# A decoder layer on one core: tile-wise waits, GpSimd diagonals and an earlier load where the opening meets the main loop

## The chip, the core and the metric

The kernel runs on one core of a Trainium2 chip. The metric is the device time of one launch in microseconds (us). The engines are TensorE (PE, with its weight loads, PEld), VectorE (DVE), ScalarE (ACT), GpSimd (POOL) and SyncE (SP), which here issues every DMA.

## What is computed

The input x has the shape 4 x 2048 x 512 (float32). The reference adds three branches to it, one after another, each on a layer norm of what came before:

```python
x = x + ssm(layernorm(x))      # y = 2 Re(z), z' = V (A z + Vinv dt x), scanned over the first axis (4 steps)
x = x + xattn(layernorm(x), ctx)   # 16 heads of 32, 77 context rows, softmax, Wq Wk Wv Wo
x = x + ffn(layernorm(x))      # W_exp (512 -> 2048), butterfly, exact gelu, butterfly, W_con (2048 -> 512)

def butterfly(y, weights, dim):          # 11 stages; stage s mixes i with i ^ 2**s
    for s in ...:
        a, b = the two halves of each pair
        y = stack(w00 * a + w01 * b, w10 * a + w11 * b)
```

The kernel folds W_exp and the first butterfly into one 512 x 2048 matrix, and the second butterfly and W_con into one of 2048 x 512. Both are then used in seven products instead of eight (Strassen's scheme in Winograd's form).

## The kernel before, in words

**Units.** The 2048 positions are cut into 16 units of 128, each with its 4 steps of the first axis, so a unit is a tile xt of 128 x 4 x 512. `front(u)` computes the first two branches and the last layer norm of a unit, as a generator of 50 steps; `feed_forward(u)` computes the third branch. In the main loop TensorE runs the products of `feed_forward(u)`, and after each of them `step()` (L649) may take a step of `front(u + 1)`: 50 steps over 102 of its 112 products.

**The up phase of a unit** has 8 pairs p of 7 products (L661, two matmuls each). TensorE's order for the first pairs is: pair 0's products 1, 6, 5 (`up_head`), then 2, 7 (`up_mid`); then for each further pair 1, 6, 5, the previous pair's 4, 3 (`up_tail`), and 2, 7. For unit 0 and p < 4 this order is fixed by hand. Product 1 of pair 0 needs only xnt; product 6 needs t2, which `combine` (L634 to L637) makes from xnt in the tile tb. Product 1 is copied out as p1 by ACT (L681), product 2 ends in a Gelu into a11 (L669, L693), product 7 in u3 and a22 (L696, L697). The weights of pair 0 are loaded in the opening (w_first, L840), those of the other pairs by L676 into one of three buffers in turn. At p = 1, x of unit u + 2 is loaded (L721). The down phase has 7 products of 8 parts each (L735).

**The opening** (L785 to L847) does three things at once: `_recurrence_taps` and `_keys_values` (small), `front(0)` (called `first`), and `_prepare` (called `prep`), which builds the two folded matrices. The order of TensorE, SyncE and GpSimd follows the program there, so the driver's `run(...)` calls and the loop at L829 set which step of `prep` goes beside which of `first`. In `_prepare`:

- `_low_products` (L186, GpSimd) and `diagonals` (L251, VectorE) make the operands of a butterfly's lower and upper stages: `bd` for the first (in the place of wo), `bdd` for the second, four of the 16 at a time between the products that need `bd`.
- L291, L303 and L315 are the TensorE stages for the first matrix. `evict` moves each bank from PSUM by VectorE (L245) or ACT (L247); six banks serve these stages in turn.
- Eight steps (L338 to L349) make the seven combinations of quarters: GpSimd L341, L342, VectorE L343, L344, and a store each (L345), with plain copies stored by L334.
- 16 steps with L355 (which reads `bdd`), then 16 with L365 and L375, make the second matrix in wdn. After every fourth of the latter, L384 to L387 combine into wup, and seven stores of 256 KB (L389) send the parts out as dn7: four sets, of which the last ends the opening. L378 loads a bias, and L391 adds it.

After `prep` x of unit 1 is loaded (L841 calls `load_x`, L418), and the biases ybias and db follow (L845, L846, added by L847 on GpSimd).

**Places.** The pool `prep` is closed at the end of the opening, and the pools of the main part (L848 to L852) take its room. In the built program, in bytes of a partition from the start of wup:

| prep | from | main part over it |
|---|---|---|
| wup, 32 KiB | 0 | x of unit 2 (xlast); a11, a12, a21 |
| wdn, 32 KiB | 32768 | a22, s1, u2d; weights 0 (pair 2); most of weights 1 (pair 3) |
| low_up, later low_dn, 15.9 KiB | 65568 | end of weights 1; tb, p1, u2, u3 |
| b1, b2, hp0 to hp3, hp_up, hp_dn | 81824 | weights 2 (pair 1), which also lie over the pool taps |

A pool opened in the place of another waits by default for all that the old pool held. Outside the opening and the fixed parts, a planner orders each engine's instructions: it goes by its own reckoning of when each will be ready, and by program order where several are. `keep_in_program_order` (keep) ties an instruction to its place among the others kept so on its engine.

Of the kernel before, what the change touches and what calls it, by code (L numbers as in the profile page):

```python
# [17 lines left out]
P = 128  # L18
# [5 lines left out]
NB = HID // P  # L24
# [142 lines left out]
def _low_products(nc, keep, low, transposed, shared):  # L167

    e, off = low[:, 0 : 2 * NB], 2 * NB
    for s in range(1, LOW):
        n = 2 ** s
        w = low[:, off : off + NB * 2 * n]
        off += NB * 2 * n
        parts = ((nc.gpsimd, slice(0, NB)),)
        if shared and s == LOW - 1:
            parts = (nc.vector, slice(0, NB // 2)), (nc.gpsimd, slice(NB // 2, NB))
        for engine, b in parts:
            v, old = (a.rearrange("p (b x) -> p b x", b=NB)[:, b] for a in (w, e))  # L180
            k = b.stop - b.start
            if transposed:
                v, old = v.rearrange("p b (x c) -> p b x c", c=2), old.unsqueeze(3).to_broadcast([P, k, n, 2])
            else:
                v, old = v.rearrange("p b (r x) -> p b r x", r=2), old.unsqueeze(2).to_broadcast([P, k, 2, n])
            keep(engine.tensor_tensor(v, v, old, ALU.mult))  # L186
        e = w
    return e.rearrange("p (b x) -> p b x", b=NB)
# [36 lines left out]
def _prepare(nc, keep, pool, room, late, banks, dram, ident, wexp_t, up_low, up_high, up_bias, dn_low, dn_high, wcon,  # L225
# [9 lines left out]
    highs, brw, spare = room  # L235
    brow = dram.tile([2, HID], F32, name="brow")
    t = wdn
# [8 lines left out]
        else:  # L246
            nc.scalar.copy(out, ps)  # L247

    def diagonals(hp, place, some=slice(0, NB)):
        for m in range(NB)[some]:  # L250
            keep(nc.vector.tensor_tensor(place[:, m, :].rearrange("p (b i) -> p b i", b=NB),  # L251
                                         hp[:, m, :].unsqueeze(2).to_broadcast([P, NB, sub]),
                                         mask.unsqueeze(1).to_broadcast([P, NB, sub]), ALU.mult))
        return [place[:, m, :] for m in range(NB)]
# [17 lines left out]
    hp = _regrouped(nc, keep, pool, hscr[0], _high_products(nc, pool, highs[:, 0], False), "hp_up")  # L272
    e = _low_products(nc, keep, low, False, True)
    hp_dn = _high_products(nc, pool, highs[:, 1], True)
    yield
    for g in range(4):
        ps = banks()
        for j in range(4):
            b = 4 * g + j
# [6 lines left out]
    for g in range(4):  # L286
        for c in range(NC):
            ps = banks()
            for j in range(4):
                b = 4 * g + j  # L290
# [5 lines left out]
    low = pool.tile([P, nlow], F32, tag="lowc", name="low_dn")  # L296
    keep(nc.sync.dma_start(out=low, in_=dn_low))
    hp_dn = _regrouped(nc, keep, pool, hscr[1], hp_dn, "hp_dn")
    bd = diagonals(hp, spare[:, 0 : NB * P].rearrange("p (m q) -> p m q", q=P))
    for m in range(NB):  # L300
        ps = banks()
        for c in range(NC):
# [2 lines left out]
        if m % 4 == 3:  # L305
            yield
    el = _low_products(nc, keep, low, True, False)
    pb = banks()
    place = late()
    for g in range(4):  # L310
        bdd = diagonals(hp_dn, place, slice(4 * g, 4 * g + 4))
        for c in range(NC):
            ps = banks()
            for j in range(4):
                nc.tensor.matmul(ps.rearrange("p (k m) -> p m k", m=4)[:, j], lhsT=t[:, 4 * g + j, c * P : (c + 1) * P],  # L315
                                 rhs=bd[4 * g + j], start=j == 0, stop=True, skip_group_check=True)
            evict(wup[:, c, :].rearrange("p (k m) -> p k m", m=NB)[:, :, 4 * g : 4 * g + 4], ps.rearrange("p (k m) -> p k m", m=4))
        for j in range(4):
            m = 4 * g + j
            nc.tensor.matmul(pb[:, m : m + 1], lhsT=bd[m], rhs=b2[:, m : m + 1], start=True, stop=True)  # L320
        nc.sync.dma_start(out=t[:, 4 * g : 4 * g + 4, :], in_=wcon.rearrange("(p m) d -> p m d", m=NB)[:, 4 * g : 4 * g + 4, :])
        yield
# [48 lines left out]
    for n, b in enumerate(order):  # L371
# [7 lines left out]
        if n % 4 == 3:  # L379
            f = slice(n // 4 * 2, n // 4 * 2 + 2)  # L380
# [15 lines left out]
def kernel(ctx: ExitStack, tc: tile.TileContext, x, ctx_t, ssm_vec, ssm_vt, ssm_vinv, wq_t, wk_t, wv_t,  # L396
                        wo_t, wexp_t, up_low, up_high, up_bias, dn_low, dn_high, wcon, b_con, down_bias, out):
    nc = tc.nc
# [17 lines left out]
    def load_x(u):  # L416
        xt = (xlast if u % 3 == 2 else xpool).tile([P, T, D], F32, tag=f"xt{u % 3}", name=f"xt{u}")
        tc.keep_in_program_order(nc.sync.dma_start(out=xt, in_=x[:, u * P : (u + 1) * P, :].rearrange("t p d -> p t d")))  # L418
        return xt

    def norm_stats(xt):

        st = small.tile([P, T, 6], F32, tag="st", name="st")
        mv = small.tile([P, T, 2], F32, tag="mv", name="mv")
        for t in (2, 3, 0, 1):
            nc.vector.bn_stats(st[:, t, :], xt[:, t, :])  # L426
            nc.vector.bn_aggr(mv[:, t, :], st[:, t, :])
        v = small.tile([P, T], F32, tag="v", name="v")
        vi = small.tile([P, T], I32, tag="vi", name="vi")
        y = small.tile([P, T], F32, tag="y", name="y")  # L430
        w = small.tile([P, T], F32, tag="w", name="w")
        nc.vector.tensor_scalar(v, mv[:, :, 1], LN_EPS, None, ALU.add)
        nc.vector.tensor_scalar(vi, v.bitcast(I32), 1, None, ALU.logical_shift_right)
        nc.vector.tensor_scalar(y.bitcast(I32), vi, -1.0, 1597463007.0, ALU.mult, ALU.add)
        nc.vector.tensor_scalar(v, v, -0.5, None, ALU.mult)
        for _ in range(3):
            nc.vector.tensor_tensor(w, y, v, ALU.mult)
            nc.vector.tensor_tensor(w, w, y, ALU.mult)
            nc.vector.scalar_tensor_tensor(y, w, 1.5, y, ALU.add, ALU.mult)
        return mv, y  # L440
# [21 lines left out]
            nc.scalar.copy(xnt[:, :, t, :], ps)  # L462
        res.append(xnt)

    def normed_pairs(xt, res):


        mv, y = norm_stats(xt)
        xpt = work.tile([P, T // 2, D // NS, P], F32, tag="xnt", bufs=2, name="xpt")
        half = D // 2  # L470
        yield
        rows = {}

        def row(n):
            i, h = divmod(n, 2)
            rows[n] = work.tile([P, NC, 2, NS], F32, tag="xn", name="xp")
            for k in range(2):
                t = 2 * i + k
                nc.vector.tensor_scalar(rows[n][:, :, k, :], xt[:, t, h * half : (h + 1) * half].rearrange("p (f n) -> p f n", n=NS),
                                        mv[:, t, 0:1], y[:, t : t + 1], ALU.subtract, ALU.mult)  # L480

        row(0)
        for n in range(T):
            i, h = divmod(n, 2)
            if n + 1 < T:
                row(n + 1)
            yield
            ps = psum.tile([P, NC, P], F32, tag="f", name="ps_t")
            for f in range(NC):
                nc.tensor.transpose(ps[:, f, :], rows[n][:, f, :, :].rearrange("p k n -> p (k n)"), ident)  # L490
            nc.scalar.copy(xpt[:, i, NC * h : NC * h + NC, :], ps)
        res.append(xpt)
# [17 lines left out]
    def front(u, xt, res, wq=None):  # L510


        got = []
        yield from normed_pairs(xt, got)
        xpt = got.pop()
        for c in range(NC):
            ps = psum.tile([P, T, P], F32, tag="f", name="ps_s")
# [122 lines left out]
    def feed_forward(u, xt, rhs, other):  # L640
# [4 lines left out]


        slot = [0]

        def step():  # L649
            slot[0] += 1  # L650
            for _ in range(slot[0] * 50 // 102 - (slot[0] - 1) * 50 // 102):
                next(other, None)

        def bank(tag):
# [71 lines left out]
        a, b, c, b7, a4 = (bank(g).rearrange("p (t d) -> p t d", t=2) for g in "abcba")  # L726
# [54 lines left out]
    xts = {}  # L781
# [3 lines left out]
    with ExitStack() as stack, tc.manual_schedule(engines={E.PE, E.SP, E.Pool}):  # L785
# [13 lines left out]
        def run(*gens):  # L799
            for g in gens:  # L800
                next(g, None)
# [6 lines left out]
        with tc.tile_pool(name="taps", bufs=1) as tp:  # L808
# [5 lines left out]
            first = front(0, xts.pop(0), ready, wq)  # L814
# [8 lines left out]
        run(prep, first, prep, first, prep, first, prep)  # L823
        nc.sync.dma_start(out=wq7, in_=wq)
        run(prep, prep, prep, prep)
        for _ in range(8):
            run(prep, first)
        run(first, first)
        for n, _ in enumerate(prep):  # L829
            if n not in (4, 8, 12, 22, 23, 24, 25, 26):  # L830
                next(first, None)
            if n == 3:
                quarter_loads(wo, wo_t, (0, 1, 2, 6))
                nc.gpsimd.tensor_tensor(wo[:, 4], wo[:, 6], wo[:, 0], ALU.subtract)
                nc.gpsimd.tensor_tensor(wo[:, 6], wo[:, 2], wo[:, 6], ALU.subtract)
                nc.gpsimd.tensor_tensor(wo[:, 5], wo[:, 2], wo[:, 4], ALU.subtract)
                nc.gpsimd.tensor_tensor(wo[:, 3], wo[:, 1], wo[:, 5], ALU.subtract)
            if n == 17:
                early.append(work.tile([P, 7, 2, P], F32, tag="pt", bufs=1, name="w_first"))
                nc.sync.dma_start(out=early[0], in_=up7[0])  # L840
        xts[1] = load_x(1)  # L841
        for _ in first:
            pass
        db = work.tile([P, D], F32, tag="xn", name="db")
        nc.sync.dma_start(out=ybias, in_=b_con.partition_broadcast(P))  # L845
        nc.sync.dma_start(out=db, in_=down_bias.partition_broadcast(P))  # L846
        nc.gpsimd.tensor_tensor(ybias, ybias, db, ALU.add)  # L847
    xlast = ctx.enter_context(tc.tile_pool(name="xlast", bufs=1))  # L848
    acts = ctx.enter_context(tc.tile_pool(name="acts", bufs=NB // 2))
    wts = [ctx.enter_context(tc.tile_pool(name=f"wts{i}", bufs=1)) for i in range(2)]  # L850
    ffn = ctx.enter_context(tc.tile_pool(name="ffn", bufs=2))
    wts.append(ctx.enter_context(tc.tile_pool(name="wts2", bufs=1)))  # L852
    loaded = [0]

    def weights(shape, name):
# [78 lines left out]
```

## Time and profile before

| what | value |
|---|---|
| median of 3 runs | 2635.3 us (2635.08 to 2636.23) |
| the profiled execution, its own time | 2635.34 us |
| its span | 2633.6 us |
| mean clock granted to TensorE | 0.995 |
| busy share PE, DVE, ACT, POOL | 97%, 55%, 31%, 36% |
| TensorE busy from 200 to 220 us | 8.76 of 20 us |
| one unit of the main loop | about 150.2 us |

The profile is of one execution. A row of a timeline gives start, length, engine, line, operation, output <- inputs, shapes, how many in a row (x4), and in brackets the idle time before it and who ended it. A row of waits says which engine at which line waited for which engine, tile and line, with us in total, how many times, and the longest. "SPq" is SyncE's queue of DMAs; "issue to landing" is the time until the data has arrived. In the table of stretches each engine has its busy time and number of instructions, then come the clock granted to TensorE (1.00 is full), the busy share of the DMA engines, and GB/s.

### The profile page before, as it was taken

The numbers are of one execution on the slowest core, as the hardware profiler recorded it, in microseconds if no ns is written. First come the engines' busy times: TensorE is split into PE (matmuls) and PEld (weight loads), VectorE is DVE, ScalarE is ACT, GpSimd is POOL, SyncE is SP. The second block draws the span as 40 slices with busy tenths as digits, with TensorE's granted clock in tenths as the row PEclk, the third lists the DMA queues.
The fourth block names the chain that finished last, engine by engine and source line by source line (L and its number), as shares of the span: only waits on it lengthen the run. The fifth ranks groups of instructions, "written<-read, shape, count | busy, mean of one in ns | idle before, by whom it ended". The sixth has DMA issues, their size and how long they took to land.

```text
span 2633.6 us, 37429 instructions
## 1 busy us (share of the span) xinstructions
PE 2565.4 (97%) x14536; PEld 2181.7 (83%) x14536; DVE 1454.5 (55%) x3349; ACT 810.9 (31%) x1472; POOL 955.2 (36%) x1029
## 2 busy tenths in 40 slices
PE   8887999999999999999999999999999999999999
PEld 5776888888888888888888888888888888888888
DVE  6766545545664564556456455545545564554541
ACT  2332414133241413324141232414124241413420
POOL 4433343515234251523425152342515234251523
PEclk9998999999999999999999999999999999999999
DMA  5546233242423324242332424233242423323243
GB/s 177 200 124 211 95 120 132 95 148 90 172 89 128 132 89 150 95 164 90 134 132 86 150 97 160 92 136 132 87 150 97 160 93 136 132 87 134 96 134 138
DMA packets 95106, 333.60 MB, mean 127 GB/s; under 512 B 15313, under 2 KB 49233, under 8 KB 77777
## 3 DMA queue, kind: packets, MB, share of 16 engines
q1 hardware_dynamic: 94930, 331.21, 35.9%
q8 instruction: 116, 1.90, 0.3%
q14 instruction: 60, 0.49, 0.1%
HBM read 297.61 MB, written 33.57 MB: 126 GB/s over the span
## 4 chain that ended last, share of the span: by engine, by line
PE 86%; DVE 7%; ACT 4%; issue 1%; DMA 1%; POOL 0%; SPq 0%; ACTq 0%; DVEq 0%; POOLq 0%
PE ps_a L735 13%; PE ps_b L664 10%; PE ps_b L735 9%; PE ps_w L505 7%; PE ps_q L505 7%; PE ps_c L664 7%; PE ps_a L664 7%; PE ps_c L735 6%; PE ps_sc L563 5%; PE ps_pt L585 4%; PE ps_s L520 3%; PE ps_o L595 2%; PE ps_t L461 2%; ACT L569 1%; DVE st L426 1%
## 5 line engine op out<-in xcount | busy, mean ns | idle before, releaser
L664 PE MATMUL ps_b<-tb,w_up 128*128 128x256 f32 x1524 | 393.7, 379 | 0.0
L735 PE MATMUL ps_a<-w_dn,a 128*128 128x256 f32 x1536 | 373.0, 380 | 0.0
L710 POOL TENSOR_TENSOR s<-a,a 128x256 f32<-128x256 f32 x128 | 93.1, 728 | 676.9 <-ACT a L669 454.5
L669 ACT ACTIVATE a<-a,hbias 128x256 f32<-128x256 f32 x384 | 193.6, 508 | 410.6 <-DVE a L705 277.5
L664 PEld LDWEIGHTS ps_b<-tb,w_up 128*128 128x128 f32 x1524 | 284.9, 190 | 38.8
L735 PEld LDWEIGHTS ps_a<-w_dn,a 128*128 128x128 f32 x1536 | 282.4, 190 | 41.6 <-issue 3.0
L664 PE MATMUL ps_a<-xnt,w_up 128*128 128x256 f32 x1016 | 260.7, 379 | 0.0
L735 PE MATMUL ps_c<-w_dn,s 128*128 128x256 f32 x1024 | 248.6, 379 | 0.0
L573 POOL TENSOR_TENSOR pr<-pr,sm 128x1232 f32<-128x1232 f32 x64 | 144.0, 2250 | 250.6 <-DVE sm L572 246.1
L462 ACT COPY xnt<-ps_t 128x512 f32<-128x512 f32 x128 | 73.8, 588 | 517.8 <-PE ps_t L461 517.8
L735 PEld LDWEIGHTS ps_c<-w_dn,s 128*128 128x128 f32 x1024 | 188.7, 190 | 27.8
L664 PEld LDWEIGHTS ps_a<-xnt,w_up 128*128 128x128 f32 x1016 | 189.6, 190 | 25.2
L613 DVE TENSOR_TENSOR xt<-ps_w,xt 128x512 f32<-128x512 f32 x96 | 66.1, 689 | 215.5 <-PE ps_w L505 148.9
L563 PE MATMUL ps_sc<-kbd,qt 128*128 128x308 f32 x512 | 173.7, 437 | 7.1 <-DVE pr L568 6.5
L723 POOL TENSOR_TENSOR xt<-xt,ybias 128x256 f32<-128x256 f32 x128 | 99.3, 811 | 223.1 <-DVE xn L452 223.0
L585 PE MATMUL ps_pt<-ident,pr 128*77 128x128 f32 x1024 | 144.8, 277 | 8.2 <-DVE pt L590 3.9
L585 PEld LDWEIGHTS ps_pt<-ident,pr 128*77 128x77 f32 x1024 | 118.2, 148 | 40.8 <-ACT a L669 11.0
L569 ACT ACTIVATE pr<-pr 128x308 f32<-128x308 f32 x256 | 111.2, 457 | 130.4 <-DVE pr L568 129.9
L505 PE MATMUL ps_q<-xnt,wq 128*128 128x256 f32 x640 | 151.1, 379 | 0.0
L505 PEld LDWEIGHTS ps_q<-xnt,wq 128*128 128x128 f32 x640 | 121.4, 190 | 16.8 <-issue 0.4
L664 PE MATMUL ps_c<-tb,w_up 128*128 128x256 f32 x508 | 131.5, 381 | 0.0
L681 ACT COPY p<-ps_a 128x256 f32<-128x256 f32 x128 | 47.7, 373 | 271.2 <-PE ps_a L664 262.5
(207 smaller groups left out, 4610.2 us busy)
## 6 DMA issues: line engine op xcount, KB each, us to landing
w_dn<-dn SPq DMA_DIRECT2D x112, 1024.0 KB, 4.8
w_up<-up SPq DMA_DIRECT2D x127, 896.0 KB, 4.6
wq<-wq SPq DMA_DIRECT2D x16, 1792.0 KB, 8.5
xt<-in_x SPq DMA_DIRECT2D x16, 1024.0 KB, 5.2
out<-xt SPq DMA_DIRECT2D x64, 256.0 KB, 4.8
wdn<-in_wexp_t SPq DMA_DIRECT2D x4, 1024.0 KB, 10.3
wdn<-in_wcon SPq DMA_DIRECT2D x4, 1024.0 KB, 4.8
up<-wo SPq DMA_DIRECT2D x8, 512.0 KB, 2.8
```

The source lines that it names most:

```text
L462: nc.scalar.copy(xnt[:, :, t, :], ps)
L505: nc.tensor.matmul(tiles[key][:, r, :], lhsT=lhs(i, r, k), rhs=rhs(i, r, k), start=key == i and r == 0 and k == 0, stop=k == 1, skip_group ...
L520: nc.tensor.matmul(ps[:, 2 * i : T, f * NS : (f + 1) * NS], lhsT=xpt[:, i, c * (P // NS) + f, :], rhs=gt[:, 0 : T - 2 * i, :], start=i == ...
L563: nc.tensor.matmul(ps[:, 0 : 4 * NK], lhsT=qt[:, g, t, :], rhs=kbd[:, t, g, :], start=True, stop=True)
L569: nc.scalar.activation(pg, pg, AF.Exp, scale=1.0 / math.sqrt(DH))
L573: nc.gpsimd.tensor_tensor(pr, pr, sm.unsqueeze(2).to_broadcast([P, NH, NK]), ALU.mult)
L585: nc.tensor.transpose(pt_ps[0:NK, j, :], pr[:, 4 * g + j, :], ident)
L664: nc.tensor.matmul(ps, lhsT=w[:, c, :], rhs=rhs[i - 1][:, c], start=first and c == 0, stop=c == 1, skip_group_check=True)
L669: nc.scalar.activation(out, x, AF.Gelu, bias=hbias[:, b : b + 1])
L710: nc.gpsimd.tensor_tensor(s1, a21, a22, ALU.add)
L723: nc.gpsimd.tensor_tensor(r, r, ybias[:, d], ALU.add)
L735: nc.tensor.matmul(ps[:, t, :], lhsT=act[p][lhs[i]][:, t, :], rhs=w[:, p, :], start=first and p == 0 and t == 0, stop=p == h - 1, skip_gro ...
```

## The change

The pools of the main part are opened with `reuse_waits="tile"`: a tile in them waits for the tiles that lay in its place, not for the whole of the old pool. `bdd` is made by GpSimd, all 16 in one go behind the low products, where VectorE made four at a time. x of unit 1 is loaded behind step n = 24 of the loop, ahead of the third and fourth set of stores, and not after the loop. The bn_stats of unit 1's first norm are kept in program order. During the first 8 products of unit 0 no step of `front(1)` is taken, and its 50 steps are spread over the 94 that follow. Two steps of `first` move behind the last two quarter steps, and the loop at L829 leaves out six of its places instead of eight.

```diff
-    def diagonals(hp, place, some=slice(0, NB)):
-        for m in range(NB)[some]:
-            keep(nc.vector.tensor_tensor(place[:, m, :].rearrange("p (b i) -> p b i", b=NB),
+    def diagonals(engine, hp, place):
+        for m in range(NB):
+            keep(engine.tensor_tensor(place[:, m, :].rearrange("p (b i) -> p b i", b=NB),
...
-    bd = diagonals(hp, spare[:, 0 : NB * P].rearrange("p (m q) -> p m q", q=P))
+    bd = diagonals(nc.vector, hp, spare[:, 0 : NB * P].rearrange("p (m q) -> p m q", q=P))
...
     el = _low_products(nc, keep, low, True, False)
+    bdd = diagonals(nc.gpsimd, hp_dn, late())
     pb = banks()
-    place = late()
     for g in range(4):
-        bdd = diagonals(hp_dn, place, slice(4 * g, 4 * g + 4))
         for c in range(NC):
...
-    def norm_stats(xt):
+    def norm_stats(xt, keep=lambda i: i):
...
-            nc.vector.bn_stats(st[:, t, :], xt[:, t, :])
+            keep(nc.vector.bn_stats(st[:, t, :], xt[:, t, :]))
...
-        yield from normed_pairs(xt, got)
+        yield from normed_pairs(xt, got, tc.keep_in_program_order if u == 1 else lambda i: i)
...
         slot = [0]
+        lead = 0 if u else 8
 
         def step():
             slot[0] += 1
-            for _ in range(slot[0] * 50 // 102 - (slot[0] - 1) * 50 // 102):
+            past = slot[0] - lead
+            for _ in range(max(past, 0) * 50 // (102 - lead) - max(past - 1, 0) * 50 // (102 - lead)):
                 next(other, None)
...
-        for _ in range(8):
+        for _ in range(6):
             run(prep, first)
-        run(first, first)
+        run(prep, prep, first, first)
         for n, _ in enumerate(prep):
-            if n not in (4, 8, 12, 22, 23, 24, 25, 26):
+            if n not in (5, 10, 22, 23, 24, 25):
                 next(first, None)
...
+            if n == 24:
+                xts[1] = load_x(1)
             if n == 17:
...
-        xts[1] = load_x(1)
...
-    xlast = ctx.enter_context(tc.tile_pool(name="xlast", bufs=1))
-    acts = ctx.enter_context(tc.tile_pool(name="acts", bufs=NB // 2))
-    wts = [ctx.enter_context(tc.tile_pool(name=f"wts{i}", bufs=1)) for i in range(2)]
-    ffn = ctx.enter_context(tc.tile_pool(name="ffn", bufs=2))
-    wts.append(ctx.enter_context(tc.tile_pool(name="wts2", bufs=1)))
+    xlast = ctx.enter_context(tc.tile_pool(name="xlast", bufs=1, reuse_waits="tile"))
+    acts = ctx.enter_context(tc.tile_pool(name="acts", bufs=NB // 2, reuse_waits="tile"))
+    wts = [ctx.enter_context(tc.tile_pool(name=f"wts{i}", bufs=1, reuse_waits="tile")) for i in range(2)]
+    ffn = ctx.enter_context(tc.tile_pool(name="ffn", bufs=2, reuse_waits="tile"))
+    wts.append(ctx.enter_context(tc.tile_pool(name="wts2", bufs=1, reuse_waits="tile")))
```

More of the change, by code (lines that the diff above doesn't have):

```diff
@@ L463, in normed, with normed_pairs @@
         res.append(xnt)
-    def normed_pairs(xt, res):
-        mv, y = norm_stats(xt)
+    def normed_pairs(xt, res, keep):
+        mv, y = norm_stats(xt, keep)
         xpt = work.tile([P, T // 2, D // NS, P], F32, tag="xnt", bufs=2, name="xpt")
```

## The prediction, as put on record before the result

> **What bounds the kernel now.** I read the waits of TensorE first, then busy time by stretch, then the timelines of the engines around each wait. In the main part TensorE itself is the bound (stretch, busy time of PE, PEld, DVE, ACT, POOL, clock, DMA share, GB/s; two of the fifteen units):
>
> ```profile
> 526.85:677.05 150.20, 148.87 (x848) 127.19 (x847) 82.95 (x196) 48.40 (x88) 52.74 (x56) 1.00 0.35 121
> 1728.45:1878.65 150.20, 148.86 (x848) 127.20 (x847) 84.17 (x196) 48.40 (x88) 51.73 (x53) 1.00 0.34 119
> ```
>
> 1.3 us of 150.2 are idle, and from unit 1 on no line is changed. So any gain lies before 262 us. Who waited for whom between 204 and 230 us (us in total, times, longest):
>
> ```profile
> PE ps_b L664 <- DMA ybias<-in_b_con: 11.2, 1, 11.2
> ACT p L681 <- DMA dn<-wup: 8.7, 1, 8.7
> DVE tb L634 <- DMA dn<-wup: 7.2, 1, 7.2
> ...
> PE ps_t L490 <- DVE xp L479: 3.6, 1, 3.6
> ```
>
> The large wait is the border between the opening and the main part. ACT, DVE and GpSimd restart together at 213.7 us, when the last store dn<-wup lands, though tb lies where low_dn lay, whose last reader (TensorE, L375) is through at 204.0. The name ybias in the first row is a late neighbour's: TensorE starts when L636 has made t2. TensorE's other wait, the last row, is for unit 1's first rows, whose x was issued only at 208.8.
>
> An earlier loss is at 87 us (start, length, instruction; first VectorE, then GpSimd, then TensorE):
>
> ```profile
> 83.04 6.67 DVE L251 TENSOR_TENSOR bd<-hp_dn,mask 128x128 f32<-128x128 f32 x4 [0.23 <-DMA hp_dn<-hscr]
> 89.63 0.68 DVE L245 COPY wup<-ps_p 128x512 f32<-128x512 f32 x1
> 79.74 9.62 POOL L186 TENSOR_TENSOR low_dn<-low_dn 128x64 f32<-128x64 f32 x6 [0.81 <-DMA low_dn<-in_dn_low]
> 90.37 4.42 PE L315 MATMUL ps_p<-wo,wdn 128*128 128x128 f32 x24 [2.92 <-DVE wup L245]
> ```
>
> Four products that take 0.28 us each elsewhere last 6.67 us, until GpSimd's six end at 89.36; the eviction queued behind them comes at 89.63, and TensorE, out of banks, stands for 2.92 us. It then runs slowly (columns as above):
>
> ```profile
> 90.40:92.00 1.60, 1.60 (x7) 1.60 (x8) 1.32 (x5) 0.00 (x0) 0.00 (x0) 0.50 0.04 10
> ...
> 216.50:218.30 1.80, 1.80 (x4) 1.48 (x5) 0.19 (x1) 0.00 (x0) 1.80 (x2) 0.50 0.97 392
> 218.30:220.10 1.80, 1.80 (x6) 1.46 (x5) 1.45 (x4) 0.00 (x0) 1.72 (x3) 0.59 1.05 392
> ```
>
> The clock is 0.50 after both waits, and at the border DMA is full. SyncE's queue there:
>
> ```profile
> 205.73 3.01 SPq L389 DMA_DIRECT2D dn<-wup  x4
> 208.83 0.68 SPq L418 DMA_DIRECT2D xt<-in_x  x1
> ...
> 213.46 0.33 SPq L676 DMA_DIRECT2D w_up<-up  x1
> 213.84 0.43 SPq L418 DMA_DIRECT2D xt<-in_x  x1
> ```
>
> [...]
>
> **GpSimd makes bdd.** VectorE loses 16 products (all of the 6.67, then three groups of 0.88), and its evictions run when their banks are full. TensorE gains the 2.92 wait and the slow clock: x24 took 4.42, where 32 take 3.68 in the chain of waits, so 24 take 2.76: 1.66. Together **-4.6**. The price on GpSimd: its 128x128 product elsewhere takes 0.428; 16 of them are 6.9 us, behind L186, from 89.4 to 96.3. Queued behind them is L341, which began at 104.42 and will be due at 99.8; GpSimd idled 15 us there. So they cost nothing; that cover is gone if one takes over (99.8 - 89.4)/16 = 0.65 us, and at 0.8 us 2.4 us of the gain go. Bounds for this part: -5 to -2.
>
> **Two of unit 0's steps later.** Two steps of the attention (scores of tile 0, an empty one) move behind the last two quarter steps, which issue GpSimd L341/L342, VectorE L343/L344 and a store each; so L341/L342 of the last quarter no longer wait behind the softmax's product L573 (126.3 to 128.5), and L573, due when VectorE has the sums at 126.2, isn't delayed by 1.5 us of quarter work at about 122. On TensorE three products of L355 (0.9 us each) instead of one stand ahead of the first transposes L585, where scores now wait 1.0 us at a time for L568. Two filled: **-1.8**, bounds -4 to +1 (an eviction that waits for the last quarter's readers could hold ACT). The skips are six instead of eight, and the lag is made up by the end. Together the opening ends 6.4 us earlier: what follows is given in new time, old time less 6.4.
>
> **x of unit 1 sooner.** One DMA of 1024 KB and 0.68 us of SyncE, moved past 14 stores of 256 KB. DMA is full there, so they land later: x took 2.0 us after the last store (213.7 to 215.7), of which a slack of about 0.8 at 190 to 202 us is used: +1.2. The last store lands at 213.7 - 6.4 + 1.2 = 208.5. The load itself lands near 196 to 199.
>
> **Waits by tile.** I take the places from the built program of before: tb and p1 lie over low_dn; a11, a12, a21 and x of unit 2 over wup; a22, s1 and the weights of pair 2 over wdn; those of pair 1 over small tiles long done. L634 can follow L391 (205.33 + 1.23), then L636: two of 0.69, then 0.2 to TensorE: 208.1 old, 201.7 new, against 216.5 (between 200.5, if L634 goes ahead of L391, and 203.5, if GpSimd blocks L636 as at 214.46). The wait of 11.2 becomes about 2.8. Now number the products of the up phase; each is 0.865 us. Products 2 to 9 end at 208.6. Product 10 needs a22, place free by about 204. Product 11 needs the copy p1 of pair 1, on ACT behind the Gelu of a11, whose place is free at 208.5: table load 1.28, Gelu 0.47 and 0.51, copy 0.37, so 211.2. 12 ends at 213. Product 13 needs pair 2's weights: they and x of unit 2 are sent after 208.5, 1.97 MB at the 0.405 MB a us of that stretch, 4.9, and about 1.3 of latency: **214.7**. Before it began at 234.2, with three groups of transposes ahead of it (0.44 each) that now come later: 232.9. Gain 18.2.
>
> That needs pair 1's weights by product 6. The old landings of w_up 1 to 3 are 5.8, 8.6 and 11.4 us after issue, the first at 219.3. Free of the border, its load can be set ahead of the last stores: nothing holds it, and the planner does such things, since at 360.9 the next unit's w_up is issued ahead of a store at 362.5 which the program has first. GpSimd's order (L635 ahead of L847) shows that it passes instructions written in order too. I take this as likeliest.
>
> **Eight products without the next unit's work.** Its steps then come at 50 in 94 products instead of 50 in 102. TensorE's sum is unchanged. x is there, so L479's rows are ready: the 3.6 us wait of L490 is gone (it is within the 18.2, and so is the slow clock). bn_stats, kept in order, comes behind L391. If denser steps uncover a softmax wait in unit 0, they cost up to 1.
>
> The sum is made against the profiled execution: 2635.34 (span 2633.6 and 1.7 around it), as good as the median 2635.3. 2635.3 - 18.2 = **2617**.
>
> **The rivals.** *Pair 1's weights stay behind the stores*, in the order written. Then the bytes ahead of them are as before: 219.3 - 6.4 - 0.8 = 212.1; TensorE stands from 205.2 for 6.9 us, runs slow (1.6), and product 13 comes at 212.1 + 6.1 + 1.6 = 219.8: gain 13.1, **2622**. For it: DMA is full. Against: the planner's habit.
> *The border stays*, tile waits doing nothing: restart at 208.5, product 2 at 211.3, product 6 at 216.5 (5.15 as before), 13 at 222.6: gain 10.3, **2625**.
> *The main loop is put in another order.* The planner orders VectorE's queue by its own reckoning, and a shifted unit 0 may set another pattern for the fifteen units after it. One more wait like that of L461 on L452 (0.97 once a unit) costs 14.6 us, two 29: 2617 + 29 = **2646**. It ends above the kernel before from 18.2/15 = 1.2 us a unit. Against: their code and idle time (1.3 us in each unit that I read) are the same throughout.
>
> **Chances.** Likeliest case 0.47 (2612 to 2620); weights behind the stores 0.26 (2620 to 2625); border stays 0.09; most of the gain given back, within 0.2%, 0.06; main loop reordered, 0.07; faster than 2611, 0.05. About 0.2%, 5 us, can be told from no change here. Faster: 0.47 + 0.26 + 0.09 + 0.05 = 0.87. The range 2611 to 2627 takes in the first three cases and leaves out the others; the bounds of the two opening parts (-5 to -2, -4 to +1) stay within it.
>
> **What would show it.** Right: no TensorE wait at L315; GpSimd's 16 products done before L341; a wait of about 3 us ahead of product 2; none of 3.6 at L490; w_up ahead of the last dn stores in SyncE's queue; units of 150.2. A wait of about 7 us at product 6 shows the first rival, one of 9 or more at product 2 the second, more than 1.3 us idle a unit the third. Wrong: GpSimd products over 0.65 us, or evictions behind a blocked ACT at 125 us.

## The result, and the profile after

| | before | after |
|---|---|---|
| median of 20 runs each, in turn on one chip | 2636.13 us (2632.25 to 2637.9) | 2631.85 us (2628.43 to 2635.04) |
| profiled execution | 2635.34 us | 2630.88 us |
| its span, its mean clock | 2633.6 us, 0.995 | 2629.1 us, 0.996 |

The ratio is 0.9983, with a 95% interval of 0.9976 to 0.999: 4.3 us faster, 0.17%. The prediction was 2617, a gain of 18.2. Up to product 2 the gain came about as foreseen, and then most of it was lost again.

Line numbers shift by one with the change (L664 is now L665, L490 is L489). Products are numbered in TensorE's order, as in the prediction: 1 to 5 are of pair 0, 6 to 8 of pair 1, 9 and 10 of pair 0 again, 11 and 12 of pair 1, 13 is the first of pair 2. Milestones of the profiled executions, in us from the span's start:

| | before | after | difference |
|---|---|---|---|
| first matmul behind the stage L315 | 104.37 | 98.10 | -6.3 |
| product 1 of unit 0 | 204.23 | 195.99 | -8.2 |
| product 2 (needs t2) | 216.50 | 200.79 | -15.7 |
| product 6 (pair 1's weights) | 221.65 | 212.88 | -8.8 |
| product 13 (pair 2's weights) | 234.2 | 221.02 | -13.2 |
| first transposes of L490, now L489 | 227.14 | 226.69 | -0.5 |
| first product of unit 1 | 376.49 | 372.40 | -4.1 |

One caution on all such tables. At 45 us, ahead of all that was changed, 32 matmuls of one line (ps_s) took 7.07 us in the profile of before and 5.40 in that of after (two lines of each):

```profile
44.38 0.63 PE L490 MATMUL ps_t<-ident,xp 128*128 128x128 f32 x4 [2.46 <-DVE xp L479]
44.84 7.07 PE L520 MATMUL ps_s<-gt,xpt 128*128 128x256 f32 x32
...
44.44 0.63 PE L489 MATMUL ps_t<-ident,xp 128*128 128x128 f32 x4 [2.12 <-DVE xp L478]
44.90 5.40 PE L519 MATMUL ps_s<-gt,xpt 128*128 128x256 f32 x32
```

The clock between 44 and 52 us was 0.79 in the one and 1.00 in the other. The profiles of all kernels here show one or the other, though nothing differs between them up to there. So up to 1.7 us of a difference between two single profiles is chance at this place.

From product 1 to unit 1 the kernel before needed 172.3 us and the kernel after 176.4. TensorE's idle time there is 16.1 us of the one (172.26 less 156.12 busy) and 15.5 of the other (176.41 less 160.95): the wait that was removed came back in other places. What makes the stretch 4.1 us longer is busy time, 160.95 against 156.12 us for the same work: TensorE ran slowly for longer (mean clock 0.95 against 0.96). The waits of TensorE between 170 and 380 us, after (total, times, longest):

```profile
PE ps_a L665 <- DMA w_up<-up: 5.5, 1, 5.5
PE ps_b L665 <- DVE tb L635: 3.8, 1, 3.8
PE ps_t L489 <- DVE xp L478: 2.9, 1, 2.9
PE ps_t L460 <- DVE xn L451: 1.5, 2, 1.0
PE ps_c L736 <- POOL s L711: 1.2, 1, 1.2
PE ps_pt L584 <- POOL pr L572: 1.0, 1, 1.0
PE ps_q L504 <- DVE tq L536: 0.2, 1, 0.2
```

Before there were two large ones, 11.2 and 3.6. Now there are three: 3.8 for t2, 5.5 for pair 1's weights, and the 2.9 for unit 1's rows, which was to go. Two small ones, L736 and L584, are new. The same in TensorE's order of time:

```profile
200.79 2.08 PE L665 MATMUL ps_b<-tb,w_first 128*128 128x256 f32 x4 [3.77 <-DVE tb L635]
...
212.88 2.08 PE L665 MATMUL ps_a<-xnt,w_up 128*128 128x256 f32 x4 [5.46 <-DMA w_up<-up]
...
226.69 0.63 PE L489 MATMUL ps_t<-ident,xp 128*128 128x128 f32 x4 [2.91 <-DVE xp L478]
```

Four matmuls of a product (1.03 us later on) take 2.08 in the first two, and 1.87 in the product behind the third (at 227.15): each of these stops is followed by slow running. The stretches of after (columns as in the prediction) show it, and the unit of the main loop below them is as it was:

```profile
522.75:672.95 150.20, 148.86 (x848) 127.20 (x847) 82.94 (x196) 48.40 (x88) 52.77 (x56) 1.00 0.35 121
200.00:220.00 20.00, 13.75 (x40) 10.99 (x41) 3.80 (x10) 3.04 (x5) 9.85 (x12) 0.66 0.88 328
210.00:215.00 5.00, 2.12 (x5) 1.76 (x6) 0.00 (x0) 0.01 (x1) 4.20 (x6) 0.51 1.04 414
```

The clock was 0.51 between 210 and 215 us, in which TensorE was busy for 2.12 us. So 13.75 us busy from 200 to 220, against 8.76 before, are in part slower work and not more of it.

Why product 6 waits stands in SyncE's queue, after:

```profile
188.94 1.79 SPq L417 DMA_DIRECT2D xt<-in_x  x1
190.83 2.45 SPq L388 DMA_DIRECT2D dn<-wdn  x3
193.33 2.70 SPq L388 DMA_DIRECT2D dn<-wup  x4
197.85 2.33 SPq L388 DMA_DIRECT2D dn<-wdn  x3
200.23 3.44 SPq L388 DMA_DIRECT2D dn<-wup  x4
203.72 0.72 SPq L847 DMA_DIRECT2D ybias<-in_b_con  x1
204.53 0.66 SPq L848 DMA_DIRECT2D db<-in_down_bias  x1
205.25 0.43 SPq L677 DMA_DIRECT2D w_up<-up  x1
```

x of unit 1 (L417) went ahead of the two last sets of stores, as written. The weights of pair 1 (L677) stand where the program has them, behind all stores and both biases. Their place was free earlier: in the built program it begins at byte 81920, past b1 (64 bytes from 81824), which L390 reads until 198.5, and the other tiles there had been done with for long.

Why the rows of L478 are late although x was loaded 20 us sooner stands in VectorE's timeline, after:

```profile
207.46 0.42 DVE L697 TENSOR_TENSOR u<-ps_b,p 128x256 f32<-128x256 f32 x1 [4.06 <-PE ps_b L665]
207.97 0.42 DVE L698 TENSOR_TENSOR a<-ps_c,u 128x256 f32<-128x256 f32 x1
216.77 0.42 DVE L685 TENSOR_TENSOR u<-ps_b,p 128x256 f32<-128x256 f32 x1 [8.37 <-PE ps_b L665]
218.63 0.42 DVE L706 TENSOR_TENSOR a<-ps_b,p 128x256 f32<-128x256 f32 x1 [1.44 <-PE ps_b L665]
218.97 0.69 DVE L425 BATCH_NORM_STATS2 st<-xt 128x6 f32<-128x512 f32 x1
...
225.81 1.38 DVE L478 TENSOR_SCALAR xp<-xt,mv,y 128x256 f32<-128x256 f32 x4
```

VectorE does nothing from 208.4 to 216.8. The bn_stats (L425), whose x had landed at 197.7, are queued behind L685, which reads product 7 of pair 1, and L706, which reads product 9; and TensorE waits for pair 1's weights at product 6. The step that issues the bn_stats is taken only after the first 8 products, so they come behind in VectorE's order. Whether their being kept in program order plays a part was not tried.

GpSimd's part went as foreseen:

```profile
78.82 8.61 POOL L186 TENSOR_TENSOR low_dn<-low_dn 128x256 f32<-128x256 f32 x4
87.38 5.87 POOL L251 TENSOR_TENSOR bd<-hp_dn,mask 128x128 f32<-128x128 f32 x16
98.15 0.73 POOL L340 TENSOR_TENSOR wo<-wup 128x256 f32<-128x256 f32 x1 [4.90 <-ACT wup L247]
```

The 16 products end at 93.25, 4.9 us before GpSimd's next work is ready. TensorE's four blocks of 32 matmuls in this stage now take 3.7 to 3.8 us each, without a wait.

### The profile page after: what moved, and what is told of

Its sections match the earlier page's. It is cut to its first block, busy times and chain, and to the rows that moved or that the text cites. A ratio compares the mean times of both kernels' runs of the same rounds, so it can differ in the third digit from the quotient of the medians.

```text
span 2629.1 us, 37413 instructions
## 1 busy us (share of the span) xinstructions
PE 2565.7 (98%) x14536; PEld 2180.5 (83%) x14536; DVE 1442.7 (55%) x3333; ACT 811.4 (31%) x1472; POOL 962.0 (37%) x1045
## 4 chain that ended last, share of the span: by engine, by line
PE 86%; DVE 7%; ACT 4%; issue 1%; POOL 1%; DMA 0%; SPq 0%; ACTq 0%; DVEq 0%; POOLq 0%
PE ps_a L736 13%; PE ps_b L665 10%; PE ps_b L736 8%; PE ps_w L504 7%; PE ps_q L504 7%; PE ps_c L665 7%; PE ps_a L665 7%; PE ps_c L736 7%; PE ps_sc L562 5%; PE ps_pt L584 4%; PE ps_s L519 3%; PE ps_o L594 2%; PE ps_t L460 2%; ACT L568 1%; DVE st L425 1%
## 5 line engine op out<-in xcount | busy, mean ns | idle before, releaser
L665 PE MATMUL ps_b<-tb,w_up 128*128 128x256 f32 x1524 | 395.5, 380 | 0.0
L736 PE MATMUL ps_a<-w_dn,a 128*128 128x256 f32 x1536 | 373.7, 380 | 0.0
L665 PEld LDWEIGHTS ps_b<-tb,w_up 128*128 128x128 f32 x1524 | 286.1, 191 | 39.4
L736 PEld LDWEIGHTS ps_a<-w_dn,a 128*128 128x128 f32 x1536 | 282.4, 190 | 41.6 <-issue 2.8
L665 PE MATMUL ps_a<-xnt,w_up 128*128 128x256 f32 x1016 | 261.9, 380 | 5.5 <-DMA w_up<-up 5.5
L736 PE MATMUL ps_c<-w_dn,s 128*128 128x256 f32 x1024 | 248.6, 379 | 1.2 <-POOL s L711 1.2
L665 PEld LDWEIGHTS ps_a<-xnt,w_up 128*128 128x128 f32 x1016 | 190.1, 191 | 31.2 <-DMA w_up<-up 5.9
L736 PEld LDWEIGHTS ps_c<-w_dn,s 128*128 128x128 f32 x1024 | 188.8, 190 | 29.4 <-POOL s L711 1.6
L584 PE MATMUL ps_pt<-ident,pr 128*77 128x128 f32 x1024 | 144.2, 276 | 8.7 <-DVE pt L589 3.3
L584 PEld LDWEIGHTS ps_pt<-ident,pr 128*77 128x77 f32 x1024 | 117.5, 147 | 41.2 <-ACT pt L587 10.3
L665 PE MATMUL ps_c<-tb,w_up 128*128 128x256 f32 x508 | 131.7, 382 | 0.0
```

What stands on the lines that cost most here:

```text
L584: nc.tensor.transpose(pt_ps[0:NK, j, :], pr[:, 4 * g + j, :], ident)
L665: nc.tensor.matmul(ps, lhsT=w[:, c, :], rhs=rhs[i - 1][:, c], start=first and c == 0, stop=c == 1, skip_group_check=True)
L736: nc.tensor.matmul(ps[:, t, :], lhsT=act[p][lhs[i]][:, t, :], rhs=w[:, p, :], start=first and p == 0 and t == 0, stop=p == h - 1, skip_gro ...
```

## The experiments

My theory after reading the trace: the opening's parts gave what the result shows; the tile waits moved the border, but pair 1's weights and unit 1's rows arrive as late as ever. The rival: the tile waits gave gain, and something else in the change (the x load among the stores, denser steps) took it back. Each kernel ran in turn with the kernel before, in three sets on three chips (medians of the kernel before 2635.2 us in all three). The change has its 20 runs from a set of its own (kernel before 2636.13), so beside medians the ratios to the kernel before are given.

**One part alone: GpSimd's products, in the kernel before.**

```diff
-        bdd = diagonals(hp_dn, place, slice(4 * g, 4 * g + 4))
...
+    bdd = diagonals(nc.gpsimd, hp_dn, late())
```

> The kernel before with one part of the change: bdd is made by GpSimd in one go. Theory: VectorE's evictions no longer stand behind products that GpSimd blocks; TensorE's stage L315 takes 17.8 us instead of 22.4 and the 4.6 us stay to the end: 2631.5 (before: 2636.1). Rival: the border is held by DMA, which is full there, and swallows what the opening gains: 2635 to 2636, with the first product of the up phase 4.6 us earlier but product 6 where it was.

Measured: 2630.65 us, ratio 0.9983 (0.9975 to 0.999). This part alone gives 4.6 us, as much as the whole change. Its stops at the border are those of before, 11.4 and 3.9 us. The 4.6 rest on the medians: the profiled execution took 2632.94 us, the longest of the 15, and in it product 2 comes 4.0 us sooner than before (212.49) but unit 1 only 2.4 (374.04), because the slow running behind L489 lasted longer (the two products behind its first stop took 1.91 us each, and 1.91 and 1.16 in the kernel before).

**One part alone: the tile waits, in the kernel before.** Only `reuse_waits="tile"` on the five pools.

> The kernel before with another part alone: the main part's pools wait tile by tile. Theory: product 2 comes at 208 us instead of 216.5, but product 6 then stands until pair 1's weights land behind the stores, x and the biases, at about 219 (before: 221.65): a gain of 2 to 3, so 2633.5. Rival (the border itself was the cost, 11.2 us): 2626 to 2628.

Measured: 2634.96 us, ratio 0.9999 (0.999 to 1.0008): no difference that can be told. Its trace shows that the waits did change. TensorE, in order of time:

```profile
210.50 2.08 PE L664 MATMUL ps_b<-tb,w_first 128*128 128x256 f32 x4 [3.63 <-DVE tb L636]
...
218.33 1.10 PE L664 MATMUL ps_b<-tb,w_first 128*128 128x256 f32 x4 [2.35 <-DVE u L684]
...
220.78 2.08 PE L664 MATMUL ps_a<-xnt,w_up 128*128 128x256 f32 x4 [1.35 <-DMA w_up<-up]
...
227.25 1.09 PE L490 MATMUL ps_t<-ident,xp 128*128 128x128 f32 x4 [2.69 <-DVE xp L479]
```

Product 2 is 6 us sooner than before (210.50 against 216.50), and L490 is where it was (227.25 against 227.14). Its rows are late for a reason of their own, which VectorE's timeline of the same kernel gives:

```profile
217.17 0.69 DVE L426 BATCH_NORM_STATS2 st<-xt 128x6 f32<-128x512 f32 x1 [6.73 <-DMA xt<-in_x]
217.78 0.41 DVE L684 TENSOR_TENSOR u<-ps_b,p 128x256 f32<-128x256 f32 x1
```

There the bn_stats wait for x itself, and L684 of pair 0 stands behind them: that is TensorE's stop of 2.35 us above. In the changed kernel they wait for their turn. Both start them within 2 us of each other, 217.2 and 219.0.

**One part undone: the change without tile waits.**

> The changed kernel without tile waits. Theory: restart at 207.6 us, product 2 at about 210.4, product 6 at about 215.6 instead of 212.9: 2.7 us slower than the changed kernel, 2634.6. Rival (tile waits carry the whole gain): 2636 or more. Second rival (what the rows of unit 1 need ends last, whatever the border does): no difference, 2632.

Measured: 2632.37 us, ratio 0.9989 (0.9982 to 0.9996), beside 0.9983 (0.9976 to 0.999) for the change: no difference that can be told. My theory at that time still gave the tile waits 2.7 us, and that was wrong. TensorE's waits in the same stretch, and two of its products:

```profile
PE ps_b L665 <- DVE tb L635: 13.5, 1, 13.5
PE ps_t L489 <- DVE xp L478: 2.8, 1, 2.8
...
215.30 1.03 PE L665 MATMUL ps_a<-xnt,w_up 128*128 128x256 f32 x4
...
217.89 1.03 PE L665 MATMUL ps_b<-tb,w_first 128*128 128x256 f32 x4
```

One wait of 13.5 stands in place of 3.8 and 5.5. Product 6 does come 2.4 us later than with tile waits (215.30 against 212.88), as the theory had it. But pair 1's weights are there by then, no stop comes before it, and products 6 to 8 run at full speed: 2.6 us, where they took 4.7 behind the stop in the changed kernel. So product 9 is level (217.89 against 217.57), and with it L706 at 218.96 (218.63 with tile waits), the bn_stats behind it at 219.30 (218.97), and L489 at 226.92 (226.69). The slow running behind a second stop used up what the tile waits had gained.

**One cause removed: unit 1's statistics ahead of unit 0's products.**

```diff
+        if u == 0:
+            next(other)
         feed_forward(...)
```

> The changed kernel, with the first step of unit 1 (its bn_stats and what follows on VectorE) taken ahead of product 1 of unit 0. Theory: bn_stats stood on VectorE behind L685 of pair 1, which waits for a product; set ahead of it, unit 1's rows are ready before their transposes, TensorE's wait of 2.9 us at L489 and the slow clock behind it (about 1.6) go: 2627.5 against 2631.9. Rival: the transposes or later products then wait for weights or for a GpSimd product, and the gain is under 1 us: 2631.

Measured: 2624.5 us, ratio 0.9955 (0.994 to 0.997), 7.4 us under the change. The bn_stats run right behind L635:

```profile
200.78 0.68 DVE L425 BATCH_NORM_STATS2 st<-xt 128x6 f32<-128x512 f32 x1
```

The wait of L489 and the 1.2 of L736 are gone, the wait for pair 1's weights is 6.9. It gave more than the 4.4 expected. In the profile TensorE's busy time from product 1 to unit 1 is 2.9 us less (158.07 against 160.95), where 1.6 had been put down for the slow running (clock from 225 to 230 us: 1.00, in the changed kernel 0.72), and L736's wait was not counted; the longer wait for the weights takes 1.4 back. The two profiles are 5.5 us apart at unit 1, so some of the 7.4 is not seen in them.

**The other cause removed: pair 1's weights early.** They are loaded in the opening, at step n = 21, into the place of qt.

```diff
+            if n == 21:
+                early.append(work.tile([P, 7, 2, P], F32, tag="qt", bufs=1, name="w_second"))
+                nc.sync.dma_start(out=early[1], in_=up7[1])
...
-                w = early.pop()
+                w = early.pop(0)
```

> The changed kernel, with pair 1's weights loaded in the opening, between the second and third set of stores' neighbours, into the place of qt (the following pairs then use the three buffers one turn earlier). Theory: product 6 no longer stands for 5.5 us; products 9 and after come about 8 us sooner, and bn_stats behind them too, so the gain stays: 2624 against 2631.9. Rival: DMA is full, so the load only pushes the last stores and pair 2's weights back by 2.3 us each, and product 13 stands instead: 2629.

Measured: 2627.63 us, ratio 0.9966 (0.9953 to 0.9979), 4.2 under the change (the two intervals overlap by 0.0003). The wait at product 6 is gone, and one of 5.4 us at product 13 has come: its weights (pair 2) are behind x of unit 2 in SyncE's queue. The bn_stats now run at 207.62, 11 us sooner, and still L489 waits 2.1 us. VectorE's timeline gives the reason:

```profile
219.05 0.42 DVE L685 TENSOR_TENSOR u<-ps_b,p 128x256 f32<-128x256 f32 x1 [7.56 <-PE ps_b L665]
219.39 0.16 DVE L431 TENSOR_SCALAR v<-mv 128x4 f32<-128x4 f32 x1
```

The next step of the same norm (L431) stands behind L685 of pair 2, which waits for product 13. The late load is another one, and it stops TensorE twice in the same way.

**Both removed.**

> Both: pair 1's weights in the opening and the first step of unit 1 ahead of product 1. Theory: product 13 at about 213 us (pair 2's weights), no wait at L489: 2616, the time that was predicted for the change. Rival: the two waits cover each other, and both together give no more than the better one, 2624.

Measured: 2621.87 us, ratio 0.9943 (0.9927 to 0.996), 10 under the change. Product 13 still waits 2.7 us. SyncE's queue of this kernel:

```profile
210.51 0.38 SPq L417 DMA_DIRECT2D xt<-in_x  x1
210.94 1.70 SPq L677 DMA_DIRECT2D w_up<-up  x3
```

1024 KB of x, which nobody needs for 150 us, are sent ahead of the weights that TensorE waits for.

**The x load put back behind the loop**, in the changed kernel.

> The changed kernel with x of unit 1 loaded behind the loop, as before. Theory: bn_stats stand on VectorE until about 219 us whatever x does, and x lands near 206, so nothing is lost: 2631.5 to 2632 against 2631.9, with the last store 2 us sooner. Rival: the earlier x is what let the rows come in time; without it 2 to 3 slower, 2634.5.

Measured: 2629.8 us, ratio 0.9979 (0.997 to 0.9988); the intervals of this and the change overlap, so no loss, perhaps a gain of 1 (by ratios) or 2 (by medians). ACT, which waits for the last store, restarts at 204.24 instead of 207.63; 1.2 of these 3.4 us are there at product 1 already (194.76 against 195.99). So moving x ahead of the stores brought nothing that shows (the bn_stats stand behind L706 here too, at 216.26) and made the stores land later.

**Steps in the old density**, 50 in 102 and not in 94.

> The changed kernel with unit 1's steps after the first 8 products at the old rate, 50 over 102. Theory: at 50 over 94 the softmax product L572 and the sums L711 on GpSimd meet, which cost TensorE 1.2 us at L736 and 1.0 at L584; at the old rate these go: 2629.8. Rival: the steps then reach beyond the last products and TensorE finishes them alone at the end of unit 0: 2632 to 2634.

Measured: 2631.53 us, ratio 0.9986 (0.9979 to 0.9993): in total not to be told from the change. In the profile, from product 1 to unit 1 it needs 175.0 us and not 176.4, and the wait of L736 is gone while that of L584 is 1.5. Of the rival 0.5 us shows: unit 1's second product waits for its tb. The profiled execution took 2637.49 us, 6 above the median of this kernel, but what was lost lies earlier: it is 0.3 us behind the changed kernel at 75 us (the transposes of L460 at 74.97 against 74.66) and 6.2 at product 1 (202.24 against 195.99), with the same program up to there.

**Statistics first, without tile waits.**

> The changed kernel with unit 1's bn_stats ahead of product 1 and without tile waits. Theory: with the rows out of the way the border shows, but pair 1's weights end the wait at product 6 either way: 213.2 us with tile waits, about 215.3 without, so 2 slower than with them, 2626.5 (with: 2624.5). Rival: the border's whole wait returns, 7 to 8 slower, 2632. Second rival: no difference.

Measured: 2628.59 us, ratio 0.9975 (0.9965 to 0.9984), 4.1 more than with them (5.3 by the ratios); the two intervals overlap by 0.0005, and of the single runs none overlap (2621.68 to 2625.62 in 4 with, 2625.71 to 2631.43 in 9 without). So the tile waits very likely have a worth once one of the two late arrivals is gone. Where it arises isn't shown: the profiled executions are the longest with and one of the shortest without, and are only 0.3 us apart at unit 1 (366.85 and 367.16).

**All loads in the order of their use.** As "both removed", and x of unit 1 ahead of the first stores, x of unit 2 behind pair 4's weights.

```diff
-            if n == 24:
-                xts[1] = load_x(1)
             if n == 17:
+                xts[1] = load_x(1)
...
-            if p == 1 and u + 2 < NU:
+            if p == (1 if u else 4) and u + 2 < NU:
```

> Pair 1's weights and bn_stats as in the run with both, and further x of unit 1 loaded before the first set of stores, where DMA is idle, and x of unit 2 behind pair 3 instead of pair 1, so that pair 2's weights don't stand behind it on SyncE's queue. Theory: the wait of 2.7 us at product 13 goes and the last stores land 2 us sooner: 2617.5 against 2621.9. Rival: DMA is full and another pair's weights end the next wait: 2621.

Measured: **2616.18 us** (2614.43 to 2616.99), ratio 0.9929 (0.9917 to 0.9942): 19.0 us under the kernel before, and the fastest version here. Against "both removed" it is 5.7 us by medians and 3.7 by ratios, whose intervals overlap, while the single runs don't. What each of the two moved loads gives was not tried. All of TensorE's waits between 170 and 380 us:

```profile
PE ps_b L665 <- DVE tb L635: 2.9, 1, 2.9
PE ps_t L460 <- DVE xn L451: 1.6, 4, 0.5
PE ps_pt L584 <- POOL pr L572: 1.0, 1, 1.0
```

And its SyncE queue, in which each load goes ahead of what can wait:

```profile
162.28 0.37 SPq L417 DMA_DIRECT2D xt<-in_x  x1
...
180.07 0.33 SPq L841 DMA_DIRECT2D w_second<-up  x1
...
202.33 1.79 SPq L677 DMA_DIRECT2D w_up<-up  x3
204.23 0.43 SPq L417 DMA_DIRECT2D xt<-in_x  x1
```

**The same without tile waits.**

> The same without tile waits. Theory: now that neither weights nor rows end the wait, the border is the last to come: product 2 about 8 us later, 6 to 8 slower than with tile waits: 2624.5. Rival: tile waits still give only 2: 2619.5.

Measured: 2624.93 us, ratio 0.9963 (0.9951 to 0.9976), 8.7 more. TensorE's large waits in it:

```profile
PE ps_b L665 <- DMA db<-in_down_bias: 9.3, 1, 9.3
...
PE ps_b L665 <- DVE u L697: 1.5, 1, 1.5
...
```

The wait that the change was made against is back, and now nothing behind it hides its cost.

**One part alone: the two steps later, and six skips**, in the kernel before.

> The kernel before, with one part: the two steps of unit 0 behind the last quarter steps, and six skips instead of eight. Theory: as the changed kernel's stages show it, 1.2 us sooner at the products with wo, of which nothing is lost after: 2634.0 (before: 2635.2). Rival: the wait for L245 on VectorE at 197 us takes it back, no change.

Measured: 2632.66 us, ratio 0.9995 (0.9987 to 1.0003): inconclusive; by medians it is 2.5 us faster, and the interval of the ratio goes from 3.4 us faster to 0.8 slower.

The worth of the tile waits by what else was late:

| | with | without | worth |
|---|---|---|---|
| kernel before | 2634.96 | 2635.23 | 0.3 |
| the change | 2631.85 | 2632.37 | 0.5 |
| statistics first | 2624.5 | 2628.59 | 4.1 |
| all loads in order of use | 2616.18 | 2624.93 | 8.7 |

The first two can't be told from nothing (the second is 1.6 us by the ratios, whose intervals overlap); the third is likely; the last is clear, with intervals that lie apart (0.9917 to 0.9942 and 0.9951 to 0.9976).

## Why the prediction was wrong, step by step

- **GpSimd's products: right, and it is nearly all that is left.** -4.6 was said. The stage L315 took 22.4 us before (81.92 to 104.37) and 17.8 after (80.32 to 98.10); alone, in the kernel before, the part gave 4.6. The 16 took 5.87 us where 6.9 was assumed, and L340 didn't have to wait for them.
- **The two steps: not settled.** -1.8 was said. The first product of wo came at 165.97 before and 159.45 after, with one product of L354 (0.9) more ahead of it; beside the 4.6, and with the 1.7 us of chance at 45 us in that pair of profiles, that leaves about 1.1 (6.5 - 4.6 - 1.7 + 0.9). The run of this part alone has an interval that holds both 0 and 1.8.
- **The border itself: right, and its time in part by luck.** Product 2 was said to come at 201.7 after a wait of about 2.8 and came at 200.79 after 3.8. Two differences nearly cancel: product 1 came 1.8 us sooner than the sum's 197.8, 1.7 of it the chance at 45 us, and L635 took 1.63 us where the sum had 0.69 (the prediction's bound of 203.5 allowed for that).
- **No slow clock behind the one wait that was to stay: wrong.** The prediction had read 0.50 after 2.92 us, and put nothing down for the running behind the 2.8 us. Products 2 to 4 took 5.3 us after it, and not 2.6. In the sum the wait for pair 2's weights would about have covered that; but with the two stops that followed it counts: TensorE's busy time up to unit 1 was 4.8 us longer than before.
- **"its load can be set ahead of the last stores ... I take this as likeliest": wrong.** The planner left pair 1's weights behind the stores and biases. Product 6 came at 212.88, where the first rival said 212.1, and product 13 at 221.02, where it said 219.8 (its wait of 6.9 was 5.5). I inferred a habit of the planner from one load that passed one store; loading the weights early by hand took 4.2 us off.
- **"x is there, so L479's rows are ready: the 3.6 us wait of L490 is gone": wrong, and this made even the first rival's 2622 too good.** The landing of x was followed, the queue of the engine that reads it was not. The sentence that followed it, "bn_stats, kept in order, comes behind L391", missed that their step is taken only after the eighth product. So they stand behind L685 and L706, which read products 7 and 9, and through these behind the very weights that are late: one late load stopped TensorE twice. Statistics first took 7.4 us off.
- **A gain at product 13 was taken as a gain at the end.** Product 13 came 13.2 us sooner and unit 1 only 4.1: before, three groups of L490's transposes had been done ahead of product 13; after, they came behind it and had their own wait to give (2.9 us), with the slow running behind that (1.87 and 1.91 us for the next two products). The prediction counted 1.3 us for them (0.44 each) and no wait.
- **x sooner, +1.2 for the stores: its cost is of that order (about 2 at ACT's restart), and no gain shows** (the run with x put back is 1 to 2 us faster, with overlapping intervals).
- **Denser steps, "up to 1":** waits of 1.2 and 1.0 us appeared at L736 and L584, together more than the 1 that was allowed; in the profile with the old density the stretch from product 1 to unit 1 is 1.4 us shorter, but in the time of the whole kernel no difference can be told.
- **The main loop:** 1.3 us idle of 150.2 in the unit read, as before, and 2256.7 us from unit 1 to the end against 2257.1; that rival was rightly put aside.

With both wrong steps repaired by hand, and x of unit 2 out of the way, the time is 2616.18 beside the 2617 that the sum gave. The repairs differ from what the sum assumed (both of x's loads were moved again), and in that profile product 13 comes at 211.68, 3.0 us before the sum's 214.7. So this says that the price of the border was about right, and the close agreement is in part luck.

What stays open is, first, why the planner keeps that load in place here and moved another at 360.9 us. The stores here belong to the opening, where SyncE's order follows the program, and those at 360.9 don't, which may be the reason; against it, GpSimd's L635 went ahead of L847 of the opening in the kernel before (213.73 and 217.39). It was not tried. Second, what the two steps and the density are worth, below the resolution of the measurement. Third, how much of the 4.3 us is the products alone, since the change (4.3) and they alone (4.6) can't be told apart.

## What to carry to other kernels

A wait removed at a border is worth only the distance to the next latest arrival, and less if a second stop and its slow running come in its place (here stops of 3.8 and 5.5 us for one of 11.2, and 4.8 us more of busy time); list everything that the next stage needs (weights, rows, statistics), and follow each through the queues it stands in: that of the DMAs (pair 1's weights, issued behind the stores and both biases, took 7.6 us to land, where the median of their line is 4.5) and that of the reading engine (x of unit 1 landed at 197.7, and its bn_stats ran at 218.97), not only to the landing of its data. When a large change moves little, test its parts alone and undone: the tile waits measured nothing that could be told in two kernels, about 4 us in a third and 8.7 in a fourth, and only the last tells what they are for. Where the DMA engines are full (their busy share was 1.00 to 1.05 in each 5 us from 205 to 225 in the kernel before), loads go in the order of their use, and that is written by hand when one can't show that a planner does it.

## What the runs showed of the hardware

- The slow clock came behind stops of very different length. In the kernel before it was 0.50 after 11.2 us of waiting and already after 2.92; in the kernel after it was 0.50 from 201 to 206 us, behind the stop of 3.77, 0.50 from 213.5 to 216, behind that of 5.46, and 0.58 from 228.5 to 231, behind that of 2.91. Four matmuls took 2.08 us behind the stops of 3.77 and 5.46, and 1.03 later on.
- For stops of about 2 us it is open whether it comes. In the 14 profiles here TensorE stops at 44 us, ahead of the 32 matmuls of ps_s. After 2.46 to 2.93 us they took 7.0 to 7.1 us, in all seven cases; after 2.04 to 2.22 us they took 5.40, in all six; but after 1.93 us ("statistics first, without tile waits") 7.07 again. The mean clock from 44 to 52 us was 0.79 in the profile of before (7.07 us) and 1.00 in that of after (5.40).
- A 128 x 128 product took 0.41 us on GpSimd (16 in a row in 5.87), and 0.28 on VectorE with GpSimd idle (16 in 3.32, from 71.36 us in the kernel before). Beside GpSimd's L186 two of VectorE's first four took much longer and ended just behind GpSimd's instruction: 2.19 us, to 85.23 (GpSimd's ended at 85.08), and 4.15, to 89.51 (89.36). L636 (at 214.46) took 1.63 us and ended at 216.09, behind GpSimd's L635 (215.55); L386, of the same shape, took 0.69 at 199.38. That GpSimd held VectorE up is read from these ends; for what reason isn't shown. With 4.9 us of idle time behind them on GpSimd, the slower engine was the right place for the 16.
- SyncE's DMAs at the border of the kernel before landed in the order of issue: the last store by 213.7 us, x of unit 1 at 215.7, ybias at 216.4, db at 217.0, pair 1's weights at 219.3, x of unit 2 at 221.9, the weights of pairs 2 and 3 at 222.9 and 226.3. Of the 4.4 us from issue to landing of w_first (896 KB, issued at 163.35) the DMA engines were busy for about 3.0 (164.2 to 167.2), which leaves about 1.4; the prediction adds 1.3 at product 13.
